# Causal attention on one core: the diagonal blocks' masks and sums are moved between TensorE, VectorE, ScalarE and GpSimd

## Chip, core and metric

The kernel runs on one core of a Trainium2 chip. The metric is the device time in microseconds (us) of one execution. Before the change the median of three runs is 3237.14 us (3230.75 to 3238.25).

## What is computed

The reference is one "macaron" layer over 2048 tokens of width 512, all in float32:

```python
x = x + 0.5 * ffn(layernorm(x))
x = x + attention(layernorm(x))     # 16 heads of 32, causal
x = x + 0.5 * ffn(layernorm(x))

# attention, for each head
scores = q @ k.T / sqrt(32)
scores = scores + triu(-inf, k=1)   # a query sees itself and what lies before it
out = softmax(scores) @ v           # then all heads together @ w_out.T + b_out
```

The feed-forward part has weights in a 4-bit code. It is not touched by the change and is left out here.

## The kernel before

**Stages.** The first feed-forward block, attention and the second one follow each other on the core. Attention runs from about 1194 to 2130 us of the span. It works on pairs of heads, p = 0 to 7, and for each pair on four blocks of 512 queries, g = 0 to 3. A step of a block takes one chunk c of 128 keys against the 512 queries: block g has 4g whole chunks and four diagonal ones, on which the mask falls. In blocks 0 to 2 the diagonal chunks come last; in block 3 they come after six whole ones and six whole ones follow (`around`). A pair so has 4 + 8 + 12 + 16 = 40 steps. A diagonal chunk computes only the queries from `off` on (0, 128, 256 or 384), so its tiles are 512, 384, 256 or 128 wide.

**Two jobs in one step.** For pair p a step computes transposed scores `ps` (keys on partitions, queries along the row), with the row maximum already subtracted: L1324 adds the negated maxima from the rows `mrow` through a matmul, L1333 adds k times q. For the pair after it, p + 1, the same step computes a tile `pm` of plain scores (queries on partitions), only to find row maxima (L1181, then the reduction L1196 on VectorE). Both heads of a pair, a = 0 and 1, have tiles of their own. The maxima of pair 0 have a stage of their own ahead of the others, from about 1205 to 1294 us. All of these tiles, and those of the projections, share seven PSUM buffers (`ps_one`); a step takes four.

**After the scores.** ScalarE takes the exponential of `ps` into the SBUF tile `pt` (L1356; there are four `pt` buffers). Two steps later TensorE multiplies it with the values (`values`, L1256). For the softmax's denominators two neighbouring steps' `pt` are first added to a tile `sum` (L1370 and L1373, two buffers), and TensorE sums that over the keys with a matmul of ones (`denominators`, L1265, also line L1256 in the profile). A block's last step has its values and the last `sum` multiplied together, two steps after it.

**The mask before.** In the maxima of pairs 1 to 7 VectorE adds a 128x128 mask to the diagonal part of `pm` (L1195) and then reduces the whole row (L1196). For pair 0 TensorE adds the mask (L1189). In `ps` ScalarE copies the diagonal 128 columns of both heads to `pt` (L1349), GpSimd masks both with one `affine_select` (L1350), and ScalarE exponentiates them in place last (L1358). In a diagonal step VectorE adds the pair's `pt`s: one copy and one addition over both heads (L1370, L1373). For whole steps GpSimd adds, one addition a head.

**The end of a block's maxima.** `finish` negates the last maximum (L1202, VectorE), splits it in three bf16 parts (L1207 and L1210, five small GpSimd instructions), and some steps later TensorE transposes them to `mrow` (L1220, L1221).

**Other work in a step.** `after_step` places pieces of the projections ("fills", L1094, L1111, L1131) behind diagonal steps, and the division of a finished block: VectorE's reciprocal (L1290) four steps after the block's last values, and in steps 8 to 11 after them GpSimd's products (L1302, two a step). Pairs 1 and 6 have no fills. In pair 0's first 16 steps GpSimd also adds the output bias to x (L1477).

**Order.** [...] In a step of the loop over `attend` that is: L1324 and L1181 for both heads, L1333 for both heads, then the maxima's masks and reductions with `finish` (`other[2]`), then `rest` of the step (exponentials, sums, the values of two steps before), then `after_step`.

Of the kernel before, what the change touches and what calls it, by code (L numbers as in the profile page):

```python
# [10 lines left out]
F32 = mybir.dt.float32  # L11
F16 = mybir.dt.float16
BF16 = mybir.dt.bfloat16
U32 = mybir.dt.uint32
I32 = mybir.dt.int32
AF = mybir.ActivationFunctionType
# [3 lines left out]
P = 128  # L20
# [15 lines left out]
def macaron_kernel(ctx: ExitStack, tc: tile.TileContext, x, packed, scales, wqk, bqk, wv, bv, wo, bo, out):  # L36
# [1004 lines left out]
    def attention(xT, xT_f, wqk_wv, next_w):  # L1041
        with tc.tile_pool(name="aw", bufs=1) as aw, tc.tile_pool(name="qk", bufs=1) as qkp, tc.tile_pool(
# [12 lines left out]

            mask_f = aw.tile([P, P], F32, tag="mask_f", name="mask_f")
            nc.gpsimd.memset(mask_f, 0.0)
            nc.gpsimd.affine_select(
                out=mask_f, in_=mask_f, compare_op=ALU.is_ge, fill=MASKED, base=0, pattern=[[-1, P]], channel_multiplier=1
            )  # L1060
            mask_b = aw.tile([P, P], BF16, tag="mask_b", name="mask_b")
            nc.gpsimd.tensor_copy(mask_b, mask_f)
            bqk_sb = aw.tile([P, 2, NQ], F32, tag="bqk", name="bqk_sb")
# [97 lines left out]
            def maxima(p):  # L1161
# [5 lines left out]
                for g in range(NB):  # L1167
# [3 lines left out]
                    for i, kb in steps:  # L1171
                        n = 512 if kb < g else (i + 1) * P
                        ps = [None, None]


                        on_pe = p == 0 and kb == g

                        def matmuls(a):
                            r = quadrant(p, a)
                            ps[a] = ps_one.tile([P, 512], F32, tag="one", name=f"pm_{p}_{g}_{i}_{kb}_{a}")  # L1180
                            nc.tensor.matmul(  # L1181
                                ps[a][:, :n], lhsT=q[r, bass.ts(4 * g + i, P)], rhs=k[r, kb * 512 : kb * 512 + n],
                                start=True, stop=not on_pe,
                            )

                        def mask():
                            if on_pe:
                                for a in range(2):
                                    nc.tensor.matmul(ps[a][:, n - P : n], lhsT=identb, rhs=mask_b, start=False, stop=True)  # L1189

                        def rest(now):
                            for a in range(2):
                                if kb == g and not on_pe:
                                    own = ps[a][:, n - P : n]
                                    nc.vector.tensor_tensor(own, own, mask_f, ALU.add)  # L1195
                                nc.vector.tensor_reduce(parts[:, a, i, kb : kb + 1], ps[a][:, :n], AX.X, ALU.max)  # L1196
                            if (i, kb) == steps[-1]:
                                finish(now)
# [26 lines left out]

                        yield matmuls, mask, rest, kb == g

            attnT = {}

            def attend(p, width):  # L1230
# [29 lines left out]

                two, summed = [], []

# [48 lines left out]
                def step(g, n, copied):  # L1311
# [28 lines left out]
                    def rest():  # L1340
                        pt = pp.tile([P, 2, 512], F32, tag="pt", name=f"pt_{p}_{g}_{c}")
                        scale = 1.0 / math.sqrt(HD)
                        plain = off
                        if c >= 4 * g:

                            plain = off + P
                            own = pt[:, :, off:plain]
                            for a in range(2):
                                nc.scalar.copy(own[:, a], ps[a][:, off:plain])  # L1349
                            nc.gpsimd.affine_select(  # L1350
                                out=own, in_=own, compare_op=ALU.is_ge, fill=MASKED, base=0,
                                pattern=[[0, 2], [1, P]], channel_multiplier=-1,
                            )
                        if plain < 512:
                            for a in range(2):
                                nc.scalar.activation(pt[:, a, plain:], ps[a][:, plain:], AF.Exp, scale=scale)  # L1356
                        if plain > off:
                            nc.scalar.activation(own, own, AF.Exp, scale=scale)  # L1358
                        two.append((pt, off))
                        if n % 2 == 1:  # L1360
                            (one, off_1), (other, off_2) = two
                            two.clear()
                            if g + 1 == NB and n + 1 == len(order(g)):

                                summed.append([(one, off_1), (other, off_2)])
                            else:
                                s = pp.tile([P, 2, 512], F32, tag="sum", name=f"sum_{p}_{g}_{n}", bufs=2)
                                eng = nc.vector if p + 1 == NPAIR or off_2 else nc.gpsimd
                                if off_1 < off_2:
                                    eng.tensor_copy(s[:, :, off_1:off_2], one[:, :, off_1:off_2])  # L1370
                                for a in range(1 if eng is nc.vector else 2):
                                    heads = slice(0, 2) if eng is nc.vector else a
                                    eng.tensor_tensor(  # L1373
                                        s[:, heads, off_2:], one[:, heads, off_2:], other[:, heads, off_2:], ALU.add
                                    )
                                summed.append([(s, off_1)])
                        pending.append(lambda args=(g, n, off, pt): values(*args))
                        if len(pending) > 2:
                            pending.pop(0)()

                    return maxrows, matmuls, rest, c >= 4 * g

# [36 lines left out]
            fill = qk[4:6] + v[:2] + qk[6:8] + v[2:]  # L1419
            for n, (matmuls, mask, rest, diagonal) in enumerate(maxima(0)):  # L1420
                for a in range(2):
                    matmuls(a)
                mask()
                rest(now)
                now += 1
                run_later(now)
                for step in norms[:2]:
                    step()
                del norms[:2]
                if n >= 4 and (n - STARTS[block_of(n)]) % (block_of(n) + 1) == 0:  # L1430
                    fill.pop(0)()
# [11 lines left out]
            for p in range(NPAIR):  # L1443
# [29 lines left out]
                for steps in attend(p, 2 if p + 1 == NPAIR else 1):  # L1473
# [5 lines left out]
                    for a in range(2):  # L1479
                        for maxrows, _, _, _ in steps:  # L1480
                            maxrows(a)
                        if other:
                            other[0](a)
                    for a in range(2):
                        for _, matmuls, _, _ in steps:
                            matmuls(a)
                    if other:
                        other[1]()
                        other[2](now)
                    for _, _, rest, _ in steps:  # L1490
                        rest()
                    for _, _, _, diagonal in steps:
                        after_step(diagonal, fill)
# [126 lines left out]
```

## Time and profile before

| What | us |
|---|---|
| median of three runs | 3237.14 |
| the profiled execution's own time | 3239.97 |
| its span | 3238.2 |
| TensorE matmuls busy | 3168.0 |
| VectorE busy | 2130.8 |
| ScalarE busy | 1063.9 |
| GpSimd busy | 1501.5 |
| pair 0's maxima, from 1194 us | 100 |
| pairs 0 to 6, from 1294.4 us | 733 |
| pair 7 with the end of attention, from 2027 us | 103 |

A group line of the profile reads: line, engine, operation, output<-inputs, shapes, count | busy us, mean ns of one | idle time of that engine ahead of these instructions, and what ended most of it. PE is TensorE, DVE VectorE, ACT ScalarE, POOL GpSimd, PEld TensorE's weight load. A line of the table by windows has the window in us, its length and then the busy us of each engine with its count of instructions, the granted TensorE clock (PEclk, 1.00 is full speed) and the DMA share. A step of a pair starts with its first L1324 matmul, so the difference of two such starts in the timeline is the time that a step takes.

### The profile page before, as it was taken

How to read it: one execution, taken by the hardware profiler on the slowest of the kernel's cores; microseconds unless marked ns; L12 is line 12 of the kernel's file. 1: busy time of each engine (PE TensorE's matmuls, PEld its weight loads, DVE VectorE, ACT ScalarE, POOL GpSimd, SP SyncE). 2: the span in 40 equal slices, each digit the busy share in tenths (PEclk: the TensorE clock that was granted, in tenths of full speed). 3: DMA queues.
4: the chain of work that ended last, by engine and by line, in shares of the span. 5: the costliest groups of instructions: out<-in, count | busy, mean ns of one | idle time of the engine just before them, and what ended most of it. 6: DMA issues, size and time to landing. Idle time of an engine off the chain costs nothing.

```text
span 3238.2 us, 44948 instructions
## 1 busy us (share of the span) xinstructions
PE 3168.0 (98%) x16496; PEld 2022.4 (62%) x16496; DVE 2130.8 (66%) x3142; ACT 1063.9 (33%) x2166; POOL 1501.5 (46%) x1541
## 2 busy tenths in 40 slices
PE   8999999999999999999999999999999999999998
PEld 4556565655656575333335433368888878888887
DVE  6666666666566555666675676677766767766675
ACT  5111111111111130454453455533333343333332
POOL 3757585766767550654553456413223222223222
PEclk9999999999999999999999999999999999999999
DMA  3222221212212200000000000054444445444441
GB/s 136 83 85 109 88 95 59 95 67 86 110 70 99 109 27 7 5 15 7 12 9 7 27 20 9 3 166 139 121 124 127 131 127 161 121 118 131 128 125 59
DMA packets 261292, 260.21 MB, mean 80 GB/s; under 512 B 21216, under 2 KB 225616, under 8 KB 257104
## 3 DMA queue, kind: packets, MB, share of 16 engines
q1 hardware_dynamic: 261072, 257.33, 24.4%
q8 instruction: 131, 2.15, 0.3%
q14 instruction: 89, 0.73, 0.1%
HBM read 176.28 MB, written 79.92 MB: 79 GB/s over the span
## 4 chain that ended last, share of the span: by engine, by line
PE 90%; DVE 5%; POOL 1%; ACT 1%; issue 1%; DMA 1%; SPq 0%; POOLq 0%; DVEq 0%; ACTq 0%
PE d_f L737 12%; PE po L438 12%; PE pg L339 12%; PE pu L339 12%; PE pod_f L866 7%; PE pm L1181 7%; PE f_f L737 6%; PE av L1256 5%; PE pqk L1094 4%; PE pof_f L866 3%; PE e_f L737 3%; PE ps L1324 2%; PE pv L1111 2%; PE poe_f L866 2%; DVE parts L1196 2%
## 5 line engine op out<-in xcount | busy, mean ns | idle before, releaser
L1196 DVE TENSOR_REDUCE parts<-pm 128x1 f32<-128x512 f32 (+3 forms) x640 | 369.8, 606 | 136.5 <-PE pm L1181 121.3
L1181 PE MATMUL pm<-kT,qT 32*128 32x512 f32 (+3 forms) x1280 | 376.3, 593 | 16.4 <-DVE parts L1196 15.0
L737 PE MATMUL d_f<-ys_f,ring 128*128 128x256 f32 x1216 | 321.4, 385 | 7.8 <-DVE o_f L770 7.8
L1356 ACT ACTIVATE pt<-ps 128x512 f32<-128x512 f32 (+3 forms) x576 | 272.0, 531 | 162.0 <-PE ps L1333 158.2
L1333 PE MATMUL ps<-qT,kT 32*128 32x512 f32 (+3 forms) x1280 | 294.3, 563 | 0.0
L737 PEld LDWEIGHTS d_f<-ys_f,ring 128*128 128x128 f32 x1216 | 228.0, 191 | 54.7 <-DVE o_f L770 22.7
L1373 POOL TENSOR_TENSOR sum<-pt,pt 128x512 f32<-128x512 f32 x154 | 192.2, 1270 | 132.7 <-ACT pt L1356 113.3
L438 PEld LDWEIGHTS po<-wd,inter 128*128 128x128 f32 x1024 | 194.8, 190 | 77.2 <-issue 55.4
L438 PE MATMUL po<-wd,inter 128*128 128x256 f32 x1024 | 241.1, 379 | 0.0
L791 DVE TENSOR_TENSOR o_f<-o_f,o_f 128x1024 f32<-128x1024 f32 x128 | 202.7, 1594 | 58.3 <-ACT o_f L776 54.7
L339 PE MATMUL pg<-xT_f,w 128*128 128x512 f32 x512 | 240.6, 598 | 0.0
L339 PE MATMUL pu<-xT_f,w 128*128 128x512 f32 x512 | 238.0, 592 | 0.0
L452 POOL TENSOR_TENSOR xq<-xq,d 128x512 f32<-128x512 f32 x124 | 161.7, 1314 | 92.8 <-DVE xq L446 56.5
L881 POOL TENSOR_TENSOR xq<-xq,d_f 128x512 f32<-128x512 f32 x48 | 64.7, 1348 | 293.3 <-DVE xq L875 227.9
L1256 PE MATMUL av<-pt,vals 128*32 128x256 f32 (+1 forms) x2432 | 194.2, 376 | 0.3 <-ACT both L1278 0.2
L791 POOL TENSOR_TENSOR o_f<-o_f,o_f 128x1024 f32<-128x1024 f32 x48 | 127.7, 2660 | 142.7 <-ACT o_f L776 141.5
L881 POOL TENSOR_TENSOR xq_second<-xq_second,d_f 128x512 f32<-128x512 f32 x45 | 61.0, 1355 | 274.3 <-DVE xq_second L875 218.7
L438 PEld LDWEIGHTS po<-wd,s 128*128 128x128 f32 x768 | 145.8, 190 | 57.7 <-issue 39.4
L438 PE MATMUL po<-wd,s 128*128 128x256 f32 x768 | 181.4, 379 | 0.0
L1256 PEld LDWEIGHTS av<-pt,vals 128*32 128x32 f32 x2432 | 53.1, 110 | 203.4 <-issue 171.1
L393 POOL TENSOR_TENSOR u<-u,u 128x512 f32<-128x512 f32 x64 | 81.7, 1277 | 211.4 <-ACT u L390 211.4
L339 PE MATMUL pg<-xsum,w 128*128 128x512 f32 x384 | 179.6, 597 | 0.0
(220 smaller groups left out, 6491.9 us busy)
## 6 DMA issues: line engine op xcount, KB each, us to landing
wd_f<-kept SPq DMA_DIRECT2D x112, 256.0 KB
kept<-wd SPq DMA_DIRECT2D x8, 1792.0 KB
xq<-in_x SPq DMA_DIRECT2D x16, 256.0 KB
pk<-in_gate_codes SPq DMA_DIRECT2D x16, 256.0 KB
sc<-in_gate_scales SPq DMA_DIRECT2D x32, 128.0 KB
pk<-in_up_codes SPq DMA_DIRECT2D x16, 256.0 KB
sc<-in_up_scales SPq DMA_DIRECT2D x32, 128.0 KB
pk<-in_down_codes SPq DMA_DIRECT2D x16, 256.0 KB
```

Of the source, the lines that this page charges most:

```text
L339: nc.tensor.matmul(ps, lhsT=a[:, j, :], rhs=b[:, j, :], start=(j == 0), stop=(j == 1))
L438: nc.tensor.matmul(ps[:, j, :], lhsT=a[i][:, k, bass.ts(2 * q + j, P)], rhs=b[i][:, k, :], start=(k == 0), stop=(k == 1),)
L452: adder.tensor_tensor(dst, dst, other, ALU.add)
L737: nc.tensor.matmul(ps[:, k, :], lhsT=fa[k][y], rhs=fb[k][y], start=first and k == 0, stop=True, skip_group_check=True,)
L791: sums.append(lambda: eng.tensor_tensor(dst, dst, other, ALU.add))
L866: nc.tensor.matmul(ps[:, j, :], lhsT=a[:, k, bass.ts(2 * q + j, P)], rhs=wd[:, PLACE[i], k, :], start=new and j == k == 0, stop=True, skip ...
L1181: nc.tensor.matmul(ps[a][:, :n], lhsT=q[r, bass.ts(4 * g + i, P)], rhs=k[r, kb * 512 : kb * 512 + n], start=True, stop=not on_pe,)
L1196: nc.vector.tensor_reduce(parts[:, a, i, kb : kb + 1], ps[a][:, :n], AX.X, ALU.max)
L1256: nc.tensor.matmul(dst_, lhsT=lhsT, rhs=rhs, start=kw.get("start", False), stop=True, skip_group_check=True)
L1333: nc.tensor.matmul(ps[a][:, off:], lhsT=k[r, bass.ts(c, P)], rhs=q[r, g * 512 + off : (g + 1) * 512], start=False, stop=True,)
L1356: nc.scalar.activation(pt[:, a, plain:], ps[a][:, plain:], AF.Exp, scale=scale)
L1373: eng.tensor_tensor(s[:, heads, off_2:], one[:, heads, off_2:], other[:, heads, off_2:], ALU.add)
```

## The change

Six edits, all within attention:

1. Maxima: mask and row maximum of a diagonal `pm` are one VectorE call, `tensor_tensor_reduce`, over the whole width, with the last `n` columns of a mask of 512. This holds for pair 0 as well, so its mask matmuls are gone.
2. Exponentials, head 0: VectorE adds a mask to the diagonal part of `ps` in PSUM, and ScalarE's exponential takes the diagonal with the rest.
3. Exponentials, head 1: as before, but the copy, the select and the exponential in place are for this head alone.
4. Sums of diagonal steps go to GpSimd for pairs 0 to 6 (pair 7 keeps VectorE), with one addition a head, and are issued at the end of the step after the one that completes the two.
5. A step's end (sums, values of two steps before) is a function of its own, `tail`, and stands behind `rest`.
6. The maxima's reduction of head 0 stands ahead of `rest`, that of head 1, with `finish`, behind it; so GpSimd's select stands ahead of the five small instructions of `finish`.

```diff
-            mask_f = aw.tile([P, P], F32, tag="mask_f", name="mask_f")
+            mask_f = aw.tile([P, 512], F32, tag="mask_f", name="mask_f")
...
+            mask_k = aw.tile([P, P], F32, tag="mask_k", name="mask_k")
...
-                        def rest(now):
-                            for a in range(2):
-                                if kb == g and not on_pe:
-                                    own = ps[a][:, n - P : n]
-                                    nc.vector.tensor_tensor(own, own, mask_f, ALU.add)
-                                nc.vector.tensor_reduce(parts[:, a, i, kb : kb + 1], ps[a][:, :n], AX.X, ALU.max)
-                            if (i, kb) == steps[-1]:
+                        def rest(a, now):
+                            most, scores = parts[:, a, i, kb : kb + 1], ps[a][:, :n]
+                            if kb == g:
+                                nc.vector.tensor_tensor_reduce(
+                                    scores, scores, mask_f[:, 512 - n :], 1.0, MASKED, ALU.add, ALU.max, accum_out=most
+                                )
+                            else:
+                                nc.vector.tensor_reduce(most, scores, AX.X, ALU.max)
+                            if a == 1 and (i, kb) == steps[-1]:
                                 finish(now)
...
-                            plain = off + P
-                            own = pt[:, :, off:plain]
-                            for a in range(2):
-                                nc.scalar.copy(own[:, a], ps[a][:, off:plain])
+                            plain[1] = off + P
+                            own = pt[:, 1, off : off + P]
+                            nc.vector.tensor_tensor(
+                                ps[0][:, off : off + P], ps[0][:, off : off + P], mask_k, ALU.add
+                            )
+                            nc.scalar.copy(own, ps[1][:, off : off + P])
                             nc.gpsimd.affine_select(
...
-                                pattern=[[0, 2], [1, P]], channel_multiplier=-1,
+                                pattern=[[1, P]], channel_multiplier=-1,
...
+                    def tail():
+                        while summing:
+                            summing.pop(0)()
                         if n % 2 == 1:
...
-                                eng = nc.vector if p + 1 == NPAIR or off_2 else nc.gpsimd
+                                eng = nc.vector if p + 1 == NPAIR else nc.gpsimd
...
+                                def add():
+                                    if off_1 < off_2:
+                                        eng.tensor_copy(s[:, :, off_1:off_2], one[:, :, off_1:off_2])
+                                    for a in range(2):
+                                        eng.tensor_tensor(s[:, a, off_2:], one[:, a, off_2:], other[:, a, off_2:], ALU.add)
+
                                 summed.append([(s, off_1)])
+
+                                if off_2:
+                                    summing.append(add)
+                                else:
+                                    add()
...
                     if other:
-                        other[1]()
-                        other[2](now)
-                    for _, _, rest, _ in steps:
+                        other[1](0, now)
+                    for _, _, rest, _, _ in steps:
                         rest()
+                    if other:
+                        other[1](1, now)
+                    for _, _, _, tail, _ in steps:
+                        tail()
```

## The prediction, made before the result was known

> **What bounds the kernel now.** I read the page first, then the stages by windows, then the chain of waits and the timeline of single steps.
>
> ```profile
> PE 3168.0 (98%) x16496; PEld 2022.4 (62%) x16496; DVE 2130.8 (66%) x3142; ACT 1063.9 (33%) x2166; POOL 1501.5 (46%) x1541
> ...
> PE 90%; DVE 5%; POOL 1%; ACT 1%; issue 1%; DMA 1%; SPq 0%; POOLq 0%; DVEq 0%; ACTq 0%
> ...
> L1196 DVE TENSOR_REDUCE parts<-pm 128x1 f32<-128x512 f32 (+3 forms) x640 | 369.8, 606 | 136.5 <-PE pm L1181 121.3
> ...
> L1373 POOL TENSOR_TENSOR sum<-pt,pt 128x512 f32<-128x512 f32 x154 | 192.2, 1270 | 132.7 <-ACT pt L1356 113.3
> ```
>
> TensorE carries the end; only where something holds it back is there time to win. Inside attention it is held back at one kind of place. Windows of pair 1, which has no fills: block 0, block 1's whole steps, its diagonal, block 2's first four steps:
>
> ```profile
> 1404.00:1411.60 7.60, 7.31 (x100) 3.17 (x96) 7.03 (x19) 5.84 (x20) 2.21 (x8) 1.00 0.00 1
> 1411.60:1425.00 13.40, 12.50 (x94) 4.44 (x92) 6.22 (x14) 5.61 (x12) 3.87 (x8) 0.75 0.05 13
> 1425.00:1433.20 8.20, 7.53 (x92) 3.20 (x88) 7.50 (x19) 5.23 (x19) 6.96 (x11) 1.00 0.05 15
> 1433.20:1443.00 9.80, 8.72 (x93) 3.32 (x91) 5.87 (x14) 4.91 (x11) 6.75 (x14) 1.00 0.01 4
> ```
>
> In the diagonals VectorE (third pair) is nearly full, 7.03 of 7.6 and 7.50 of 8.2. The four whole steps behind a diagonal take 13.4 and 9.8 us. By the timeline's L1324 starts such steps take 2.39, 5.77, 3.26, 1.94: the second is held, the third runs at half clock. The chain tells why, here behind block 2:
>
> ```profile
> 1459.53 0.19 DVE nmax L1202
> ...
> 1459.84 0.23 POOL split L1207
> ...
> 1461.20 0.34 POOL pt L1350
> ...
> 1461.57 0.42 ACT pt L1358
> ...
> 1462.02 0.42 DVE sum L1373
> 1462.44 0.61 DVE parts L1196
> ...
> 1463.10 0.69 PE pm L1181
> ```
>
> A loop through four engines: the late VectorE finishes the maxima, GpSimd's five pieces stand ahead of the select, ScalarE's exponential waits for the select, VectorE's sum waits for that, the reductions stand behind the sum, and TensorE's next `pm` needs their PSUM buffers. Pair 4, whose diagonals are filled with projections, shows the steps unheld: second to fourth together 5.9 us. Over 5.9, the others lose (pairs 0, 1, 2, 3, 5, 6): behind block 0 2.8, 5.1, 5.0, 1.8, 4.9, 5.1; behind block 1 2.4, 1.8, 3.4, 1.9, 3.4, 5.1; behind block 2 3.4, 3.3, 1.8, 1.9, 3.4, 1.8. Sum 58 us; behind block 3 nothing is lost. Diagonals in pairs 1 and 6 take 7.6 to 8.2 where TensorE alone needs 6.4 (2.22+1.49 there, 1.65+1.01 for the two narrow steps in pair 2): 11 us more over eight blocks.
>
> [...] ScalarE's read takes 186 to 188. [...]
>
> **The change part by part.**
>
> *Fused mask and maximum.* Removed: 224 masks of 291. The fused instruction passes all elements once, so I take the reductions' times (685, 556, 423, 290 by width; L1196 by form) and 130 for the accumulator read. Ends: it can't be under the reduction alone, so the read's lower end is 0 and no gain lies below; upper end 186, as on ScalarE[...]. *Head 0's mask* adds one VectorE instruction a diagonal step, 291 like L1195 (same shape, PSUM, mask). ScalarE's exponential of head 0 now waits for it, and behind that the step's other exponentials; it stands behind one fused instruction, so it is done about 1 us after `ps`, against 0.53 (two copies of 267) that ScalarE spent there; ScalarE is 5.2 of 8.2 busy and hides it.
>
> VectorE in a diagonal (four steps): before, reductions 3.91 + masks 8x0.291 + sums (two copies 0.6, 1.04, 0.43) = 8.3 us and waits for ScalarE. After: 3.91 + 8x0.13 + 4x0.29 + 0.2 = 6.3 us with no wait but TensorE's. That fits into 6.4. So the loop is cut, and VectorE's part of the losses goes: 58, and 9 of the 11.
>
> *Sums to GpSimd.* This is the new load. L293 shows 128x384 at 1.0 us; L1302, 128 wide, 0.50; one copy of 256 I take at 0.42 like the select (0.41; ends 0.3, the cast of 128, and 0.65). So the sum of the first two diagonal steps is 0.42+2x1.0 = 2.45, of the last two 0.42+2x0.5 = 1.45. The select of one head is 0.3 (292, ident's). GpSimd's queue as it is issued, from the third diagonal step's copy on: select, first sum, [products L1302], select, five small pieces 1.4, [products], last sum. With gaps of 0.05 to 0.1: 1.3 (matmuls and copy) + 0.35+2.55+0.35+1.4+1.5 = 7.4 us after that step's start, and 9.5 with the two products (1.05 each). Products fall into the diagonals of blocks 1 and 2, not of block 0. The trace before, the diagonal of block 1:
>
> ```profile
> 1425.28 2.50 POOL L1373 TENSOR_TENSOR sum<-pt,pt 128x512 f32<-128x512 f32 x2 [3.75 <-ACT pt L1356]
> 1427.73 0.41 POOL L1350 TENSOR_SCALAR_AFFINE_SELECT pt<-pt 128x256 f32<-128x256 f32 x1
> 1428.10 0.97 POOL L1302 TENSOR_TENSOR attnT<-both,den 32x128 f32<-32x128 f32 x2
> ...
> 1435.99 2.18 POOL L1302 TENSOR_TENSOR attnT<-both,den 32x128 f32<-32x128 f32 x4
> ```
>
> It shows 6.96 of 8.2 busy before anything is added. Who waits: TensorE multiplies the last sum in the second whole step, 1.3 us after its start. Unheld, that is after the third diagonal step's start: pairs 0, 1, 2, 6 1.65+1.01+2.05+1.3 = 6.0 (block 0: 6.4); pairs 3 and 5 8.2 (8.5); pair 4 13. New waits: block 0: pairs 1, 2, 6 1.0; 3, 5 none; pair 0 with two bias additions of 1.28 3.6. Blocks 1, 2: pairs 0, 1, 2, 6 3.5 (0.5 more in 1 and 6, whose queue is still busy with the whole step's sum of 2.5, and in block 1 of pair 0, by its bias additions); pairs 3, 5 1.3. Net gain over the lists above: block 0: -0.9+4.1+4.0+1.8+4.9+4.1 = 18; block 1: -1.7-2.2-0.2+0.6+2.1+1.1 = -0.3; block 2: -0.2-0.8-1.7+0.6+2.1-2.2 = -2.2. Sum 15.5. With the 9 of the diagonals 24.5. In block 3 of pairs 0, 1, 2, 6 the last select stands behind the first sum, and ScalarE's exponentials behind that: about 0.8 each, -3.
>
> *Pair 0's maxima.* The 32 mask matmuls are 3.7% of the chain over these 89 us: 3.3 saved, VectorE (55 of 100) hides the reads.
>
> *Pair 7.* Sums stay on VectorE, a step later; 16 masks of 0.29 and a few 0.07 for split additions, 5 us among 68 of 103: 0, within 3 either way. The longer mask's memset is one instruction of GpSimd, under the first feed-forward block's end.
>
> *Sum.* 24.5-3+3.3 = 25 less, with the other things at 0: 3240.0-25 = 3215. The profiled execution is 2.8 over the median, so 3212.
>
> **The rivals.**
>
> *GpSimd does not bind* (its last sum is ready when needed, because the queue runs ahead). Then the full 58+9+3 go: 3167. For it: GpSimd is 54 of 89 us busy in pair 1. Against: 3.9 us of sums a block more, placed in the densest stretch; hence partly, 3170 to 3195.
>
> *VectorE stays the bound*: the fused operation takes two cycles an element. Diagonals then need 6.3+4x2x0.33 = 8.9, as before; the loop through GpSimd is still cut, but half of block 0's gain and the diagonals' 9 are lost: 3230. Against it: one mask and one maximum fit in one pass by the reductions' own rate.
>
> *Slower: GpSimd's last sum.* Same place, TensorE's product with the last sum. Each us more there costs in 18 blocks (not in pair 4's). At 1.9 us later a block the 25 gained turn into 10 lost, the point at which it is slower by 0.3%; at 2.4 it gives 3255. That needs the 8.2 us from select to last sum (with the products) about a quarter slower than taken[...].
>
> **How the numbers follow.** Likeliest 0.46, 3203 to 3226; GpSimd free 0.20; VectorE bound 0.16; slower 0.18. About 0.3%, 10 us, is what a measurement of this kernel can tell from no change. Faster: 0.44+0.20+0.05 = 0.69; same 0.13; slower 0.18. The range takes in most of the second case, all of the third and the start of the last: 3170 to 3245.
>
> **What would show it.** Right: no VectorE wait for ScalarE in pairs 0 to 6; fused instructions at 0.68 for 512 with a short read; second whole steps behind block 0 near 3; GpSimd about 3.4 us a block busier (3.9 less four selects' 0.12), and TensorE waiting there for GpSimd's `sum` behind blocks 1 and 2. Wrong: a fused instruction over 1 us, second steps all near 2 (GpSimd free), or over 7 (slower).

## The result and the profile after

| | median us | range | of so many runs |
|---|---|---|---|
| before | 3234.39 | 3230.75 to 3238.25 | 4 |
| after | 3198.86 | 3197.13 to 3200.64 | 4 |

The ratio is 0.989, with a 95% interval of 0.9873 to 0.9907: the change takes 35.5 us off. The profiled execution of after took 3200.64 us, its span is 3198.9, 39.3 less than the span of before. The prediction's sum, made against the profiled execution, was 25 less. The profiled execution of before took 5.6 us more than its median, so differences between these two traces are a few us larger than those between the medians.

The page after, the lines that answer to those shown of before:

```profile
PE 3127.4 (98%) x16464; PEld 2006.0 (63%) x16464; DVE 2061.4 (64%) x3209; ACT 1048.0 (33%) x2070; POOL 1577.4 (49%) x1710
...
PE 91%; POOL 3%; DVE 2%; ACT 1%; issue 1%; DMA 1%; SPq 0%; POOLq 0%; ACTq 0%; DVEq 0%
...
L1195 DVE TENSOR_REDUCE parts<-pm 128x1 f32<-128x512 f32 x384 | 246.6, 686 | 159.5 <-PE pm L1183 159.1
```

In the chain VectorE fell from 5% to 2% and GpSimd rose from 1% to 3%: one holder of TensorE has partly been put in the place of another. Where the 39.3 us are, by the first matmul of each pair in the two timelines: pair 0's maxima end at 1290.2 instead of 1294.4 (4.2 less), pairs 0 to 6 take 698.7 instead of 732.6 (34.0 less, unrounded), pair 7 up to its last step 3.9 less, and what follows took 2.8 more, nearly all of it in stages that the change does not touch (over all the traces below, this last stretch takes 1128 to 1134 us).

The windows of pair 1 again: block 0, block 1's whole steps, its diagonal, block 2's first four steps.

```profile
1401.90:1409.00 7.10, 6.89 (x103) 2.90 (x99) 5.28 (x21) 5.10 (x16) 3.32 (x11) 1.00 0.01 3
1409.00:1417.26 8.26, 8.26 (x97) 3.50 (x95) 5.53 (x13) 5.64 (x12) 6.18 (x13) 1.00 0.07 19
1417.26:1423.73 6.47, 6.47 (x96) 2.72 (x93) 5.47 (x22) 4.63 (x15) 5.81 (x11) 1.00 0.05 13
1423.73:1434.54 10.81, 8.84 (x93) 3.38 (x91) 4.98 (x12) 5.08 (x11) 9.78 (x21) 1.00 0.03 8
```

Block 1's whole steps, behind block 0, fell from 13.4 to 8.26 us and TensorE (first pair) is busy throughout. The diagonal fell from 8.2 to 6.47, and VectorE (third pair) has room in it. But the four steps behind block 1's diagonal went from 9.8 up to 10.81, and there GpSimd (fifth pair) is busy for 9.78 of them. The chain of waits in that last window:

```profile
1428.50 0.45 POOL attnT L1301
...
1429.02 0.41 POOL sum L1378
...
1429.47 0.41 PE av L1255 x2
```

GpSimd's queue for the same stretch (timeline; start and length in us), from the first sum's additions on, without the five small pieces of `finish` and the copies:

```profile
1423.34 1.96 POOL L1380 TENSOR_TENSOR sum<-pt,pt 128x384 f32<-128x384 f32 x2
1425.25 0.97 POOL L1301 TENSOR_TENSOR attnT<-both,den 32x128 f32<-32x128 f32 x2
1426.29 0.29 POOL L1351 TENSOR_SCALAR_AFFINE_SELECT pt<-pt 128x128 f32<-128x128 f32 x1
...
1427.98 0.97 POOL L1301 TENSOR_TENSOR attnT<-both,den 32x128 f32<-32x128 f32 x2
...
1429.37 0.87 POOL L1380 TENSOR_TENSOR sum<-pt,pt 128x128 f32<-128x128 f32 x2
```

TensorE had finished the values by 1427.5 and stood still until the copy that begins the last sum was done, at 1429.42. That is the wait that the prediction named. All waits of TensorE's weight loads of this kind, over pairs 0 to 6 (in total us, times, longest), first before, then after:

```profile
PEld pm L1181 <- DVE parts L1196: 41.9, 29, 2.8
```

```profile
PEld av L1255 <- POOL sum L1378: 19.9, 9, 2.4
...
PEld av L1255 <- POOL sum L1380: 9.7, 30, 1.1
```

### The profile page after: what moved, and what is told of

It reads as the page before. It is cut to its first block, busy times and chain, and to the rows that moved or that the text cites. A ratio compares the mean times of both kernels' runs of the same rounds, so it can differ in the third digit from the quotient of the medians.

```text
span 3198.9 us, 45147 instructions
## 1 busy us (share of the span) xinstructions
PE 3127.4 (98%) x16464; PEld 2006.0 (63%) x16464; DVE 2061.4 (64%) x3209; ACT 1048.0 (33%) x2070; POOL 1577.4 (49%) x1710
## 4 chain that ended last, share of the span: by engine, by line
PE 91%; POOL 3%; DVE 2%; ACT 1%; issue 1%; DMA 1%; SPq 0%; POOLq 0%; ACTq 0%; DVEq 0%
PE d_f L737 12%; PE po L438 12%; PE pu L339 12%; PE pg L339 11%; PE pod_f L866 7%; PE av L1255 6%; PE f_f L737 6%; PE pm L1183 6%; PE pof_f L866 3%; PE pqk L1099 3%; PE e_f L737 3%; PE ps L1323 2%; PE pv L1116 2%; PE poe_f L866 2%; PE pp L1136 2%; PE ps L1332 1%
## 5 line engine op out<-in xcount | busy, mean ns | idle before, releaser
L1195 DVE TENSOR_REDUCE parts<-pm 128x1 f32<-128x512 f32 x384 | 246.6, 686 | 159.5 <-PE pm L1183 159.1
L1357 ACT ACTIVATE pt<-ps 128x512 f32<-128x512 f32 (+3 forms) x608 | 288.0, 528 | 179.2 <-PE ps L1332 132.1
L1183 PE MATMUL pm<-kT,qT 32*128 32x512 f32 (+3 forms) x1280 | 335.5, 579 | 0.2
L1380 POOL TENSOR_TENSOR sum<-pt,pt 128x512 f32<-128x512 f32 (+2 forms) x266 | 271.3, 1042 | 66.3 <-ACT pt L1357 64.4
L1332 PE MATMUL ps<-qT,kT 32*128 32x512 f32 (+3 forms) x1280 | 281.5, 540 | 0.0
L1255 PE MATMUL av<-pt,vals 128*32 128x256 f32 (+1 forms) x2432 | 190.1, 370 | 0.5 <-ACT both L1277 0.4
L339 PE MATMUL pu<-xsum,w 128*128 128x512 f32 x384 | 177.7, 592 | 0.0
```

The lines of the kernel that those rows point to most:

```text
L339: nc.tensor.matmul(ps, lhsT=a[:, j, :], rhs=b[:, j, :], start=(j == 0), stop=(j == 1))
L1183: nc.tensor.matmul(ps[a][:, :n], lhsT=q[r, bass.ts(4 * g + i, P)], rhs=k[r, kb * 512 : kb * 512 + n], start=True, stop=True,)
L1195: nc.vector.tensor_reduce(most, scores, AX.X, ALU.max)
L1255: nc.tensor.matmul(dst_, lhsT=lhsT, rhs=rhs, start=kw.get("start", False), stop=True, skip_group_check=True)
L1332: nc.tensor.matmul(ps[a][:, off:], lhsT=k[r, bass.ts(c, P)], rhs=q[r, g * 512 + off : (g + 1) * 512], start=False, stop=True,)
L1357: nc.scalar.activation(pt[:, a, plain[a] :], ps[a][:, plain[a] :], AF.Exp, scale=scale)
```

## The experiments

The theory that I went in with is the prediction's: the loop through four engines is cut because VectorE no longer makes the diagonal sums; GpSimd's lateness is the price of it. The rival: the order of issue (select ahead of the five pieces, edit 6) cuts the loop by itself, and moving the sums only costs. Both can be true of the loop; what they differ in is whether the sums have to move. A second question was what the fused operation and head 0's mask are worth.

To compare runs I use the working of the prediction on each trace: "behind" is the time of the second to fourth steps behind blocks 0, 1 and 2 over 5.9 us, summed over pairs 0, 1, 2, 3, 5, 6; "diagonals" is the time of the eight diagonals of pairs 1 and 6 over 6.37 us each, what TensorE alone needs for them; both, and the time of pairs 0 to 6, from the starts of the step's first matmul in one trace of each kernel. Times are medians; ratios are to the runs of before made along with each.

| kernel | median us | ratio, 95% interval | behind | diagonals | pairs 0 to 6 |
|---|---|---|---|---|---|
| before | 3234.4 | | 58.3 | 11.5 | 732.6 |
| after | 3198.9 | 0.989, 0.9873 to 0.9907 | 32.5 | 2.8 | 698.7 |
| e1_split | 3203.7 | 0.9896, 0.9877 to 0.9915 | 32.5 | 5.9 | 705.2 |
| e2_order | 3205.3 | 0.990, 0.9884 to 0.9916 | 34.1 | 3.2 | 703.1 |
| e3_sums_at_once | 3168.7 | 0.9789, 0.9774 to 0.9805 | 0 | 7.6 | 669.4 |
| e4_sums_later | 3179.0 | 0.9821, 0.9805 to 0.9836 | 0.7 | 2.3 | 677.8 |
| f1_order_alone | 3175.3 | 0.9816, 0.9801 to 0.983 | 0.1 | 13.0 | 678.3 |
| f2_fused_alone | 3210.4 | 0.992, 0.9905 to 0.9935 | 41.2 | 10.1 | 711.4 |
| f3_mask_alone | 3240.2 | 1.0017, 1.0008 to 1.0026 | 36.4 | 18.5 | 735.6 |
| e6_products | 3177.6 | 0.9819, 0.9802 to 0.9835 | 8.8 | 9.6 | 679.5 |
| e5_direct | 3173.9 | 0.9809, 0.9789 to 0.9829 | 1.0 | 2.5 | 673.3 |
| f6_no_mask | 3170.8 | 0.980, 0.978 to 0.9819 | 1.1 | 10.1 | 673.3 |
| g1_direct | 3169.7 | 0.9797, 0.9777 to 0.9816 | 0 | 7.1 | 670.4 |
| g2_nomask_direct | 3171.1 | 0.980, 0.9781 to 0.9819 | 0 | 9.9 | 673.1 |

### e1_split: the fused operation taken apart

```diff
-                                nc.vector.tensor_tensor_reduce(
-                                    scores, scores, mask_f[:, 512 - n :], 1.0, MASKED, ALU.add, ALU.max, accum_out=most
-                                )
+                                own = ps[a][:, n - P : n]
+                                nc.vector.tensor_tensor(own, own, mask_f[:, 3 * P :], ALU.add)
+                                nc.vector.tensor_reduce(most, scores, AX.X, ALU.max)
```

> The changed kernel with the fused mask and maximum taken apart again (VectorE adds the mask to 128 columns, then reduces). Theory (the loop through four engines was cut by moving the sums and by putting the select ahead of finish; the fused operation only shortens the diagonals): VectorE needs 7.6 us a diagonal in place of 6.4, which shows in pairs 1 and 6 only, 1.2 us in eight blocks at most: 3204 to 3210. Rival (the gain is VectorE's relief by the fused operation): 25 us or more are lost, 3224 and up.

Measured 3203.67 us (3202.81 to 3204.36), 4.8 over after: just under the theory's range, and the rival is out. The losses behind the diagonals are the same 32.5; the diagonals of pairs 1 and 6 cost 3.1 more. With the sums on GpSimd the fused operation is worth about 5 us, and it does not touch what holds TensorE.

### e2_order: `finish` ahead of `rest` again

```diff
                         other[1](0, now)
+                        other[1](1, now)
                     for _, _, rest, _, _ in steps:
                         rest()
-                    if other:
-                        other[1](1, now)
```

> The changed kernel with both heads' maxima and finish ahead of rest again, so GpSimd's five pieces stand ahead of the last select. Theory: VectorE is no longer late, so the pieces cost the select only their own 1.4 us plus a short wait for the last maximum, and the sum comes later by that wait alone; 0 to 0.6 us a block in 18 blocks: 3199 to 3210. Rival (the order was what cut the loop): the waits behind block 0 come back, 20 us or more: 3220 and up.

Measured 3205.31 us (3202.57 to 3205.62), 6.5 over after, 1.6 of it behind the diagonals: the theory's range, and the rival is out. Behind block 0 the loss is 4.7 us (4.0 of it in pair 0) instead of the 24.6 of before. So the loop is open here although the select again stands behind the five pieces. The diagonal of pair 1's block 0 shows why: VectorE is at the next step's maxima before the select has begun.

```profile
1410.07 0.22 POOL L1206 CAST split<-left 128x8 bf16<-128x8 f32 x1
1410.21 0.29 POOL L1351 TENSOR_SCALAR_AFFINE_SELECT pt<-pt 128x128 f32<-128x128 f32 x1
```

```profile
1408.99 1.29 DVE L1195 TENSOR_REDUCE parts<-pm 128x1 f32<-128x512 f32 x2 [0.46 <-PE pm L1183]
```

Where the sums are on GpSimd the order of select and pieces matters little: whichever comes first, the last sum comes behind both.

### e3_sums_at_once: the diagonal sums back on VectorE, without the delay

```diff
-                                eng = nc.vector if p + 1 == NPAIR else nc.gpsimd
+                                eng = nc.vector if p + 1 == NPAIR or off_2 else nc.gpsimd
...
-                                if off_2:
+                                if off_2 and p + 1 == NPAIR:
```

> The changed kernel with the diagonal steps' sums of pairs 0 to 6 on VectorE and in the step itself, as in the kernel before, but one addition a head. Theory: TensorE's waits for GpSimd's sums behind blocks 1 and 2 (about 28 us) go, but VectorE waits for ScalarE's exponential again and has 8.5 us a diagonal, so behind all blocks of pairs 1, 3, 5, 6 it is late: 3205 to 3220. Rival (the sums' place does not matter, the fused operation does): within 5 us of the changed kernel or faster by the full 28, 3170.

Measured 3168.71 us (3168.45 to 3169.68): 30 us less than after, and 36 below the low end of what I expected. What fell here is that the sums have to leave VectorE: with the select ahead of the pieces they need not. (The rival's 3170 came true, but the run with the order alone, below, comes near it without the fused operation.) Behind every diagonal the loss is gone; only the diagonals of pairs 1 and 6 got 4.8 us longer in all, because VectorE's first sum stands ahead of the next maxima. VectorE's timeline in the diagonal of pair 1's block 2 (1.56 us of sums, then head 0's maximum of the third diagonal step without a gap):

```profile
1435.87 1.56 DVE L1380 TENSOR_TENSOR sum<-pt,pt 128x384 f32<-128x384 f32 x2
1437.35 0.42 DVE L1191 CUSTOM_DVE_ANT_0 pm<-pm,mask_f 128x256 f32<-128x256 f32 x1
```

So moving the sums to GpSimd costs 30 us net in this kernel. This is the best of all versions measured, though some below can't be told from it.

### e4_sums_later: the sums on VectorE, but with the delay

```diff
-                                eng = nc.vector if p + 1 == NPAIR else nc.gpsimd
+                                eng = nc.vector if p + 1 == NPAIR or off_2 else nc.gpsimd
```

> As the run before it, sums of diagonal steps on VectorE, but a step later as in the change. Theory: no wait for ScalarE on VectorE, only 2.1 us more work a diagonal; the 28 us of waits for GpSimd go, pairs 1 and 6 lose up to 2 us in eight blocks: 3180 to 3195, faster than the changed kernel. Rival (VectorE's load was the old bound, not the wait): pairs 1 and 6 and those with output projections fall back to the old steps, 3210 and up.

Measured 3178.95 us (3177.98 to 3180.26): 1 us below the range expected, and 10 over the run with the sums at once. The delay shortens the diagonals of pairs 1 and 6 (2.3 against 7.6), but the first whole step behind a diagonal grows, in pairs 0 and 2 to between 2.8 and 4.1 us, where it takes 2.0 to 2.3 with the sums at once. In block 0 of pair 2 the delayed sum (from 1509.96, 1.28 us) stands in VectorE's queue ahead of the last diagonal step's maxima, which end at 1511.95, and in the chain of waits two `pm` matmuls of the first whole step fill 1510.97 to 1512.25. That these stretch because the maxima hold their buffer is read from those times; the trace marks no such wait there. So of edit 4's 30 us the delay alone brings 10, when VectorE makes the sums.

### f1_order_alone: only edits 5 and 6

From the run with the sums at once on VectorE, the fused operation is taken apart as in e1_split, and both heads' masks go the way of before:

```diff
-                            plain[1] = off + P
-                            own = pt[:, 1, off : off + P]
-                            nc.vector.tensor_tensor(
-                                ps[0][:, off : off + P], ps[0][:, off : off + P], mask_k, ALU.add
-                            )
-                            nc.scalar.copy(own, ps[1][:, off : off + P])
+                            plain = [off + P, off + P]
+                            own = pt[:, :, off : off + P]
+                            for a in range(2):
+                                nc.scalar.copy(own[:, a], ps[a][:, off : off + P])
...
-                                pattern=[[1, P]], channel_multiplier=-1,
+                                pattern=[[0, 2], [1, P]], channel_multiplier=-1,
```

Three small things stay as after, here and in the next two runs: pair 0's masks in the maxima are on VectorE (3 to 4 us less than before in that stage), a diagonal sum is one addition a head, and pair 7 keeps its delayed sums and edit 5 (4 us less).

> Of the change only the order: head 1's maximum and finish behind rest, with the end of a step behind that. Masks as in the kernel before (VectorE adds and reduces, pair 0 too; ScalarE copies both heads, GpSimd selects both), sums of diagonal steps on VectorE at once. New theory (the select ahead of finish cuts the loop, since the exponential no longer waits for the last maximum): the waits behind block 0 to 2 fall by half or more, VectorE's 8.3 us a diagonal stays: 3195 to 3212. Rival (VectorE's relief by the fused operation cuts it): little, 3225 to 3240.

Measured 3175.27 us (3173.97 to 3179.07): 59 us less than before, more than I had expected of either theory; 54 of it in pairs 0 to 6. The losses behind the diagonals are 0.1 us instead of 58.3, although VectorE does all its old work, at 2146.9 us busy over the span even 16 more than before. Before, in the diagonal of pair 1's block 1, the last sum waited on VectorE (the bracket is the idle time and what ended it), since the select stood behind the pieces:

```profile
1436.39 0.43 DVE L1373 TENSOR_TENSOR sum<-pt,pt 128x256 f32<-128x256 f32 x1 [2.10 <-ACT pt L1358]
```

```profile
1434.22 0.22 POOL L1207 CAST split<-nmax 128x8 bf16<-128x8 f32 x1 [1.53 <-DVE nmax L1202]
...
1435.50 0.41 POOL L1350 TENSOR_SCALAR_AFFINE_SELECT pt<-pt 128x256 f32<-128x256 f32 x1
```

With the order alone, GpSimd's queue and then VectorE's at the same place:

```profile
1419.05 0.41 POOL L1349 TENSOR_SCALAR_AFFINE_SELECT pt<-pt 128x256 f32<-128x256 f32 x1 [1.02 <-ACT pt L1348]
1419.86 0.22 POOL L1206 CAST split<-nmax 128x8 bf16<-128x8 f32 x1 [0.41 <-DVE nmax L1201]
```

```profile
1419.93 0.49 DVE L1378 TENSOR_TENSOR sum<-pt,pt 128x128 f32<-128x128 f32 x2
```

The select no longer waits for the maxima that VectorE is still finishing: it starts at 1419.05, its wait ended by ScalarE's copy; VectorE ends the maxima at 1419.80, and its sum follows at 1419.93 without a wait, so the exponential is done by then. Nothing of the loop is left to be cut by less work on VectorE.

### f2_fused_alone: only edit 1

The run with the sums at once on VectorE, with the order as in e2_order and both heads' masks as in f1_order_alone:

```diff
                         other[1](0, now)
+                        other[1](1, now)
...
-                    if other:
-                        other[1](1, now)
```

> Of the change only the fused mask and maximum; order, ScalarE's and GpSimd's masks and the sums on VectorE at once as in the kernel before. New theory (order): the loop stands, VectorE is 1.2 us a diagonal earlier: 3215 to 3230. Rival (VectorE's relief): most of the gain of the kernel with the sums left on VectorE, 3175 to 3195.

Measured 3210.41 us (3205.09 to 3212.27), 24 less than before and 5 under what the new theory gave; the rival is out. In the traces pair 0's maxima have 4.2 of the gain, pair 7 has 3.9 and pairs 0 to 6 have 21. The loss behind the diagonals falls from 58.3 to 41.2: a shorter VectorE queue ends the same loop earlier, without opening it.

### f3_mask_alone: only edits 2 and 3

The run with the sums at once on VectorE, with the fused operation apart as in e1_split and the order as in e2_order:

```diff
+                                nc.vector.tensor_tensor(own, own, mask_f[:, 3 * P :], ALU.add)
+                                nc.vector.tensor_reduce(most, scores, AX.X, ALU.max)
...
+                        other[1](1, now)
```

> Of the change only head 0's mask on VectorE with one select of head 1; order, separate mask and maximum and sums on VectorE at once as in the kernel before. New theory (order): VectorE gets 1.2 us a diagonal more, the loop stands: 3230 to 3250. Rival (the shorter select and copies on GpSimd and ScalarE cut the loop): 3215 or less.

Measured 3240.23 us (median of 12, 3231.68 to 3245.45), ratio 1.0017 (1.0008 to 1.0026). The profiled execution was its fastest. The second to fourth steps behind the diagonals gain 22 us, but other steps give it back: the diagonals, with the added VectorE work, take 15 us more (7 of it in pairs 1 and 6), and the first step behind them, which that sum leaves out, 9 more (in pairs 1 and 2 it takes 2.3 to 3.8 us where it took 2.0 to 2.4). Pairs 0 to 6 together take 3 us more. Head 0's mask alone is no gain.

### e6_products: the change with GpSimd's products four steps later

```diff
-                            at((2 if direct else 8) + j, lambda j=j: chunk(j))
+                            at((2 if direct else 12) + j, lambda j=j: chunk(j))
```

(and a third `both` buffer, which the products read for longer)

> The changed kernel with GpSimd's products of the division four steps later (12 to 15 behind a block's last values, a third buffer for what they read), so that none falls into a diagonal or the two steps behind it. If TensorE waits for GpSimd's last sum because the products stand ahead of it: the second steps behind blocks 1 and 2 fall from near 5 us to under 3, 15 to 25 us faster than the changed kernel, 3174 to 3184. Rival (the sums themselves are too slow for the place): under 6 us, 3193 to 3199.

Measured 3177.55 us (3175.35 to 3179.95), 21 less than after, as the first theory expected. Behind blocks 1 and 2 the loss falls from 28.1 to 4.7; behind block 0 it stays at 4.2, nearly all in pair 0, where bias additions (L1487) stand in GpSimd's queue and no product was moved. GpSimd's queue in pair 1 behind block 1 now:

```profile
1420.71 0.29 POOL L1351 TENSOR_SCALAR_AFFINE_SELECT pt<-pt 128x128 f32<-128x128 f32 x1
...
1422.22 0.40 POOL L1378 COPY sum<-pt 128x256 f32<-128x256 f32 x1
1422.58 0.86 POOL L1380 TENSOR_TENSOR sum<-pt,pt 128x128 f32<-128x128 f32 x2
1423.41 0.97 POOL L1301 TENSOR_TENSOR attnT<-both,den 32x128 f32<-32x128 f32 x2
```

The copy follows the select by 1.5 us, after by 2.7, and the products come behind the sum. So what held TensorE was the products' place in GpSimd's queue, not GpSimd's total load: the edit moves its instructions and takes none away. The later place has a price of its own: in block 2 of pairs 1 and 6 the third diagonal step takes 4.4 and 4.8 us instead of 1.8. In pair 1 a whole step's sum and two products now stand ahead of the select in GpSimd's queue; ScalarE's exponential comes behind the select, and from 1290 to 2000 us TensorE's weight loads of L1255 wait for such exponentials twice, 5.0 us in all, where the trace of after lists no such wait.

### e5_direct: the change without the last sum

```diff
-                            if g + 1 == NB and n + 1 == len(order(g)):
+                            if g + 1 == NB and n + 1 == len(order(g)) or off_2 == 3 * P:
```

> The change, but the last two diagonal steps of a block in pairs 0 to 6 are not added to a sum: TensorE multiplies their two tiles with the ones one by one, as it does already in the last steps of block 3. So GpSimd has no last sum to make, and TensorE has one more narrow product of ones a head in those blocks. Theory (the change gains its time by the order of issue, and gives part of it back where TensorE waits for GpSimd's last sum behind a diagonal): the waits behind blocks 0, 1 and 2 go, and TensorE pays about 0.1 to 0.3 us a block for the added products, so 3170 to 3185, near the run with the products later (3177.6). Rival (the waits come from GpSimd's whole load, and the whole steps' sums behind the diagonal will be late in their place): 3190 to 3202.

Measured 3173.89 us (3171.59 to 3178.33): 25 less than after; behind the diagonals the loss is 1.0 instead of 32.5. Had GpSimd's whole load been the cause, the next sums, of whole steps, would have been late instead; all waits of TensorE's weight loads for GpSimd's sums fell from 29.6 us in after to 5.3 (1290 to 2000 us). But this run also takes 33 us of work from GpSimd in pairs 0 to 6 (465.0 to 432.1), so it is e6_products, with the same load, that tells place from load. What TensorE's 128 added matmul instructions cost is seen better in g1_direct, at 1 us within the ranges of the runs.

### f6_no_mask: the sums at once on VectorE, both heads' masks as before

The diff to e3_sums_at_once is that of f1_order_alone:

```diff
+                            plain = [off + P, off + P]
+                            own = pt[:, :, off : off + P]
+                            for a in range(2):
+                                nc.scalar.copy(own[:, a], ps[a][:, off : off + P])
```

> The run with the diagonal sums at once on VectorE (3168.7), but with both heads' masks as before the change: two copies by ScalarE, one select of GpSimd over both, exponentials in place. Theory A (VectorE's mask of head 0 costs there what it costs alone, and frees ScalarE and GpSimd of nothing that is on the path): some 2 to 4 us faster, 3164 to 3168, with the last diagonal step of pairs 1 and 6 falling from 2.1 towards 1 to 1.5, since VectorE has 0.3 us less in each diagonal step. Theory B (head 0's mask on VectorE takes it off the longer way over ScalarE, GpSimd and ScalarE, which then holds the sums): slower, 3172 to 3180.

Measured 3170.82 us (3168.75 to 3173.65). Both theories missed: the two intervals overlap, so the times tell nothing apart. The trace says that theory A's reason was wrong. The last diagonal step of pairs 1 and 6 did not fall from 2.1 but rose to 2.3 to 2.5 (1.24 in block 0), because VectorE's first sum now waits for the longer way over GpSimd and ScalarE:

```profile
1436.61 1.29 DVE L1378 TENSOR_TENSOR sum<-pt,pt 128x384 f32<-128x384 f32 x2 [0.75 <-ACT pt L1357]
```

Theory B named that way rightly, but put more on it than it costs: the medians differ by 2.1 us, pairs 0 to 6 of the traces by 3.9. Beside f1_order_alone, from which it differs by the fused operation alone, it is 4.5 us faster: again about 5 us for edit 1.

### g1_direct: the sums at once on VectorE, without the last one

The edit of e5_direct, made in e3_sums_at_once:

```diff
+                            if g + 1 == NB and n + 1 == len(order(g)) or off_2 == 3 * P:
...
+                                eng = nc.vector if p + 1 == NPAIR or off_2 else nc.gpsimd
```

> The run with the diagonal sums at once on VectorE (3168.7), and in it the last two diagonal tiles of a block multiplied with the ones directly, without a sum. VectorE loses a copy of about 0.3 and an addition of about 0.4 us in the last diagonal step, TensorE gets one more narrow product a head. Theory (in pairs 1 and 6 VectorE sets the length of the last diagonal step, 2.1 instead of 1.0): 1 us less in up to 6 blocks, against 0.1 to 0.3 us of TensorE in some 21 blocks: 3162 to 3169. Rival (TensorE's added products weigh more than what VectorE saves): 3169 to 3174.

Measured 3169.65 us (3169.11 to 3173.41): 1 us over e3_sums_at_once, with overlapping ranges, so no difference that can be seen. That lies in the rival's range, but in no way that tells it from no effect. In blocks 1 and 2 the last diagonal step of pairs 1 and 6 stays at 1.6 to 2.1, since it is the first sum that stands ahead of the maxima there, as e3's two lines show, and not the last.

### g2_nomask_direct: both

The edits of f6_no_mask and g1_direct together:

```diff
+                            plain = [off + P, off + P]
...
+                            if g + 1 == NB and n + 1 == len(order(g)) or off_2 == 3 * P:
```

> Both of the two edits before at once: sums at once on VectorE, both heads' masks over ScalarE and GpSimd, last two diagonal tiles multiplied directly. If the two gains are of the same stretch (VectorE in the last diagonal steps) they do not add up: 3160 to 3167, no better than the better of the two by more than 2 us. If the masks' longer way matters (theory B of the run before): slower than the run with the direct product alone by 3 us or more.

Measured 3171.13 us (3170.7 to 3173.36). That is slower than either gain would have it, and 1.5 us over g1_direct instead of the 3 or more of theory B: neither came true. Probably nothing adds up because little is left: in pairs 0 to 6 of e3_sums_at_once TensorE is busy for 665.5 of 669.4 us. That is not shown, since busy time is no lower bound: before, with the same matmuls, it was 710.3 of 732.6.

## Why the prediction was right in the time, and what it left out

The measured 3198.9 us lies 13 under the prediction's 3212, below its likeliest case (3203 to 3226) and above its first rival (3170 to 3195). It was right by its range, 3170 to 3245, which is wide enough to hold no change at all. The terms below erred nearly all the same way, by too little gain; they did not cancel.

**The fused operation: right.** By width 695, 563, 429 and 295 ns, predicted 685, 556, 423, 290; the accumulator read takes 142 (130 taken, my estimate between 0 and the 186 of ScalarE's read in before). VectorE's rows of after:

```profile
L1191 DVE CUSTOM_DVE_ANT_0 pm<-pm,mask_f 128x512 f32<-128x512 f32 x64 | 44.2, 695 | 11.5 <-PE pm L1183 11.1 <-PE ps L1332 0.4
...
L1347 DVE TENSOR_TENSOR ps<-ps,mask_k 128x128 f32<-128x128 f32 x128 | 41.1, 326 | 3.1 <-PE ps L1332 3.1
L1191 DVE DVE_READ_ACCUMULATOR2_ANT parts<- 128x1 f32 x256 | 36.2, 142 | 0.0
```

The plain reduction of 512 columns takes 686 in the same trace (L1195), so mask and maximum together cost 9 ns more than the maximum alone. The rival with two cycles an element is out: at the 1.03 ns a column that the reductions of before show ((685-290)/384), a second pass over 512 columns would have brought it to about 1210, by an estimate. Head 0's mask takes 326 ns, not the 291 of L1195 before: 112 of the 128 come right behind an accumulator read and take 332, the other 16 take 290, and in e1_split, which has no such reads, the mean is 289.

**VectorE waits no more for ScalarE: right.** Before, in pairs 0 to 6 (VectorE's waits), and after, the longest ones:

```profile
DVE sum L1373 <- ACT pt L1358: 44.6, 24, 2.4
```

```profile
DVE parts L1195 <- PE pm L1183: 142.8, 168, 5.3
DVE pm L1191 <- PE pm L1183: 43.1, 41, 4.0
```

All that VectorE waits for now is TensorE, but for 0.9 us. That holds in e2_order too, so it does not rest on edit 6. The diagonals of pairs 1 and 6 gave 8.7 us (11.5 to 2.8); predicted 9.

**GpSimd's last sum: right in kind, 10 us too dear.** The lists of the prediction leave 18.3 us behind block 1 and 17.9 behind block 2; measured are 14.9 and 13.2. Behind block 0 it leaves 6.6 and the trace 4.3: pair 0 loses 4.1 (3.6 predicted), the others nothing (1.0 each). So the gain there is 58.3-32.5 = 25.8, predicted 15.5. The queue itself was sized well: from the third diagonal step's start (1420.92 in pair 1, block 1) to the last sum's end (1430.24) it took 9.3 us, and 9.5 was taken. What was wrong is the wait at its end, 2.7 for a predicted 4.0. TensorE came to the product 6.58 us after that start, not 6.0: the steps were 0.28 longer, and the values took until 1.6 us into the second whole step, not 1.3. And it did not wait for the whole sum: its first products read only columns that the copy fills, so it began at 1429.47, 0.8 us before the sum was complete. GpSimd became 76 us busier in pairs 0 to 6 (389.0 to 465.0), 2.7 a block where 3.4 were taken.

**The rest of the sum.** Block 3: -3 was predicted and nothing was lost; in pair 1 ScalarE waited 2.41 us for the last select, and TensorE was busy for all of the 11 us from 1466 to 1477. Pair 0's maxima: 4.2, predicted 3.3. Pair 7: 3.9 less, predicted 0 within 3. Edit 6 has no part in that, because pair 7 makes no maxima; f1_order_alone and f2_fused_alone, which there differ from before only by edit 5 and the delayed, split sums, gain the same 3.9. Together: 24.8 + 10.3 + 3 + 0.9 + 3.9 - 0.3 (diagonals) - 0.5 (the other steps of pairs 0 to 6) - 2.8 (after pair 7's last step) = 39.3, as the spans have it. The 2.8 is not explained; over the fourteen traces that stretch varies by 6 us.

**The half clock.** Behind block 0 of pair 1 the clock of before is 0.50 from 1417 to 1423 us; that covers the third step of the prediction, and the trace marks no idle time of TensorE over 0.67 us ahead of it there. In after TensorE stands still for 1.96 us ahead of its product with the last sum, behind block 1 of that pair, and the clock is 1.00 from 1423 to 1437 us. So a wait of TensorE was not enough to bring the half clock about; what did is not shown.

**What it left out: the order alone.** The prediction worked out that VectorE, relieved of the sums, fits its diagonal work under TensorE, "so the loop is cut". For the change that is sound: e2_order, which has all edits but the sixth, has no VectorE wait for ScalarE and almost no loss behind block 0. But it took this for the only way. It counted edit 6 only as an order in GpSimd's queue and gave it no price. The runs give it one: alone it takes the losses behind the diagonals from 58.3 to 0.1, with VectorE as laden as before. So the loop has two places at which it opens: the select, queued on GpSimd behind five others that waited for VectorE, and VectorE's sum, which waits for what the select releases. Less VectorE work around them does not open it (edit 1 alone leaves 41.2, edits 2 and 3 alone 36.4). Edit 4 alone was not run; that it, and not edits 1 to 3 together, opens the loop in e2_order is argued from the queues and not shown.

GpSimd's two queues under f1_order_alone show the swap: before, the first piece starts at 1434.22 and the select at 1435.50; with the order alone, the select starts at 1419.05 and the first piece at 1419.86. With the loop open by the order, moving the sums only puts them into a queue in which TensorE waits for them: 30 us, more than four fifths of what the change itself gains.

**The rivals.** "GpSimd does not bind" (3167) was the time that the change would have had without its own edit 4: 3168.7. The slower case needed the 8.2 us from the select to the last sum a quarter longer; in pair 1's block 1 they took 7.5 (1422.73 to 1430.24).

## What to carry to other kernels

Before an engine is relieved of work because it stands in a chain of waits, look at which instruction in that chain waits in a queue for something that it does not need, and give the order of issue a price of its own: here it was worth all of a 58 us loss, and no instruction was added for it. Work that is moved to an engine with time to spare is late if it lands behind work that nobody waits for (21 us here, after against e6_products); read the queue of the receiving engine at that place, not its busy share (49% here), and either put the work that is waited for first or do without it. Price edits one at a time, and once each alone: the edits act on the same loop, and their gains do not add (in pairs 0 to 6 the fused operation 21 us alone, the order 54 alone, both 59).

## What the runs showed of the hardware

- A masked row maximum in one VectorE instruction with an operand in PSUM and one in SBUF costs what the maximum alone does (695 ns for 512 columns, 686 for the plain reduction, both in after), and 142 ns for reading the accumulator out, in place of 291 for the mask before.
- GpSimd's cost of small operations next to each other, in after: 456 ns for an addition of 128x128, 999 for 128x384, 1272 for 128x512, 398 for a copy of 128x256.
- Less waiting came with a higher granted clock of TensorE: 0.987 over the span of before, 0.993 after, 0.996 where the losses behind the diagonals are gone (e3_sums_at_once).
